# Turning x1 and x2 in the FP4 stage: TensorE transposes against a trip through DRAM and VectorE's square transposes

## The chip, the cores and the metric

The kernel runs on one core of a Trainium2 chip. The metric is the device time of one execution in microseconds (us). A separate profiled execution gives the trace. TensorE is called PE (its weight loads PEld), VectorE DVE, ScalarE ACT, GpSimd POOL; SP is the engine whose queue issues nearly all transfers.

## The reference

The program is two transformer layers on 2 x 1024 tokens of 512 channels, float32. Each layer adds an attention and a feed-forward part to x and normalizes after each. Cut to the part that the change touches:

```python
x = layernorm(x + linear_attention(x))            # gives x1
w_gu, w_dn = dequant(gate_up), dequant(down)      # 4-bit codes times fp16 scales of 128 inputs each
g, u = split(x @ w_gu.T)                          # 1408 features each
y = (silu(g) * u) @ w_dn.T
x = layernorm(x + y / rms(y))                     # gives x2
x = layernorm(x + gated_linear_attention(x))      # second layer
x = layernorm(x + top_k_ffn(x))
```

x1 enters the FP4 product, and x2 enters the second layer's products, with the channels on the partitions. The layer norms leave both with the tokens on the partitions. So both have to be turned.

## The kernel before, in words

Tokens are worked on in four blocks of 512, each four tiles of 128 tokens by 512 channels (`x_t[blk]`, in SBUF all the time). The program has stages, one after the other: the first attention (`s1`, to about 236 us of the trace), the FP4 feed-forward (to about 500 us), the second attention, and the top-k feed-forward.

**First attention.** The order of PE, DVE, ACT and POOL is made by a scheduler from the program's dependences. In the gaps the FP4 weights are unpacked: `unpack` issues a transfer of packed codes (`pk`, L267, two buffers), DVE shifts and masks them (L270, L271), and ACT writes them out as weights (`wgu`, `wdn`, L274). Each transfer waits until ACT has freed its buffer. `o_products(blk)` ends with the layer norm of a block; its last step, a subtraction and a multiplication per tile, runs on POOL (L222). Block 0's x1 is turned by PE inside this stage (`split_some`); that stays.

**FP4 feed-forward.** Here the order of PE, DVE, ACT and POOL is written out by hand (`manual_schedule`). The work is cut into chunks: chunk n is block n // 11 and a group n % 11 of 128 features, 44 in all. x1T is held as two float32r numbers, `x1Th` (rounded) and `x1Tl` (the remainder), and each 128-channel piece of a product is two matmuls, one with each (`in_two`, L928). A chunk has four pieces k for the gate and four for the up part. After each of the first three pieces the sum in PSUM is multiplied by a ratio of scales (L953 on ACT, L955 on DVE), and the next piece adds to it. The last piece of the gate goes through Silu (L957); the last of the up part is multiplied with it on DVE into `whole` (L959). POOL splits `whole` into `hhi` and `hlo` (L961, L962), which are the weights of the down product `yp`; after each group DVE multiplies `yp` by a ratio (L987).

Step n of the loop has two halves, and two chunks are in work at once. In each half PE runs, in this order: the older chunk's gate piece, the newer chunk's gate piece, the older chunk's up piece, the newer chunk's up piece (two matmuls each), and two `yp` products (four matmuls). A list `later` holds further work by step and half, which is issued after the `yp` products of that half: the row statistics and the norm of x2 (`Normed`, stats on DVE, norm on POOL), for the block that has just ended.

The dictionary `turned_in` names the steps in which PE turns a tile, in the second half, before the `yp` products: four transposes of 128 x 128 into a gate bank (`transposed`, L236). For x1 ACT then copies the rounded part (L250) and DVE subtracts it to get the remainder (L251): steps 4 to 7 for block 1, 17 to 20 for block 2, 28 to 31 for block 3. For x2 ACT copies the tile to xT (L1050): steps 22, 23, 32, 33 for block 0 and 34, 38, 39, 40 for block 1. Where a tile was turned, the next step's first half does the newer chunk's gate piece after the up pieces, since the bank is still in use. Blocks 1, 2 and 3 are first wanted by chunks 11, 22 and 33, in the first half of the step of that number.

**SP's queue** runs in the program's order; a transfer whose source or room isn't ready holds all behind it. Eight completion counters are used in turn, so a transfer also waits for the eighth one before it. At the end of `s1` SP issues the 11 broadcasts of the down ratios (`ratio`, L913).

Of the kernel before, what the change touches and what calls it, by code (L numbers as in the profile page):

```python
# [10 lines left out]
F32 = mybir.dt.float32  # L11
F32R = mybir.dt.float32r
F16 = mybir.dt.float16
# [8 lines left out]
P = 128  # L22
B, T, C = 2, 1024, 512
NB = 4
KC = C // P
I_FF = 1408
NI = I_FF // P
# [5 lines left out]
FG = 2 * NI  # L33
# [40 lines left out]
def body(ctx: ExitStack, tc: tile.TileContext, a: dict, out: bass.AP):  # L74
    nc = tc.nc
# [7 lines left out]
    dram = ctx.enter_context(tc.tile_pool(name="dram", bufs=1, space=DRAM))  # L83
# [9 lines left out]
    def mm_bank(name):  # L93
        return bank("mm", name)

    def acc_bank(name):
        return bank("acc", name)

    fp4 = ctx.enter_context(ExitStack())
    wfp4 = fp4.enter_context(tc.tile_pool(name="wfp4", bufs=1))  # L100
# [20 lines left out]
            wdn[i] = wfp4.tile([P, wdn_parts[i + 1] - wdn_parts[i], C], F32R, tag=f"wdn{i}", name=f"wdn{i}")  # L121
        return wdn[i][:, g - wdn_parts[i]]

    gus = wfp4.tile([KC * FG, P], F16, name="gus")
    scale = wfp4.tile([P, KC * FG], F32, name="scale")


# [2 lines left out]
    def const(name):  # L130
        at, n = _AT[name]
        return table[:, at : at + n]
# [3 lines left out]
    def place_w(i, name):  # L136
        return wpool.tile([P, KC, C], F32, tag=f"A{i}", name=name)
# [4 lines left out]
    x_t = [x[:, :, :C] for x in x_row]  # L142
# [4 lines left out]
    def xT_slot(i, name, dtype=F32):  # L147
        return xtp.tile([P, KC, 512], dtype, tag=f"xT{i}", name=name)

    def new_xT(blk):  # L150
        t = xT_slot(blk % 2, f"x0T{blk}")
        return t, a["xT"][:, blk * 512 : (blk + 1) * 512].rearrange("(k p) t -> p k t", p=P)
# [12 lines left out]
    t, src = new_xT(0)  # L165
# [15 lines left out]
    xT = {0: t}  # L181
# [33 lines left out]
    def layernorm(x, mv, eps=1e-5, by=nc.vector):  # L215

        n = x.shape[1]
        rs = sp.tile([P, 4], F32, tag="rs", name="rs")
        nc.vector.tensor_scalar_add(rs[:, :n], mv[:, :, 1], eps)  # L219
        power = nc.gpsimd.tensor_tensor(rs[:, :n], rs[:, :n], const("mhalf")[:, :n], ALU.pow).ins  # L220
        for i in range(n):
            by.tensor_scalar(x[:, i], x[:, i], mv[:, i, 0:1], rs[:, i : i + 1], ALU.subtract, ALU.mult)  # L222
        return power
# [8 lines left out]
    def transposed(x, name, room=mm_bank):  # L232

        pt = room(name)
        for k in range(KC):
            ins = nc.tensor.transpose(pt[:, k * P : (k + 1) * P], x[:, k * P : (k + 1) * P], ident).ins  # L236
        last_turned[0] = ins
        return pt

    def split_tiles(blk):  # L240

        i, j = ((2, 2), (1, 0), (0, 1), (2, 2))[blk]
        hi = xT_slot(i, "x1Th", F32R)
        lo = wpool.tile([P, KC, 512], F32R, tag=f"A{j}", name="x1Tl")
        return hi, lo

    def split_quarter(parts, blk, i, room=mm_bank):
        hi, lo = (t[:, :, i * P : (i + 1) * P] for t in parts)
        pt = transposed(x_t[blk][:, i], "x1Tp", room).rearrange("p (k t) -> p k t", k=KC)
        nc.scalar.copy(hi, pt)  # L250
        nc.vector.tensor_sub(lo, pt, hi.bitcast(F32))  # L251
# [7 lines left out]
    s1 = ctx.enter_context(ExitStack())  # L259
    wk = s1.enter_context(tc.tile_pool(name="s1", bufs=2))  # L260
    dq = s1.enter_context(tc.tile_pool(name="dq", bufs=2))

    def unpack(parts_, packed, n):

# [26 lines left out]
    def unpack_some(n):  # L291
        for _ in range(n):
            job = next(to_unpack, None)
            if job is not None:
                with tc.issue_after(anchor[0]):
                    unpack(*job)
# [46 lines left out]
    def behind():  # L343

        return ExitStack() if last_pe[0] is None else tc.issue_after(last_pe[0])
# [68 lines left out]
    tile_of = lambda i: slice(i * P, (i + 1) * P)  # L414
# [119 lines left out]
    def o_products(blk):  # L534

        A11, A12, A21, A22 = (qT[blk][:, 2 * e : 2 * e + 2, 256 * t : 256 * t + 256] for t in range(2) for e in range(2))
        G = G_of[blk // 2]
        B11, _, B21, B22 = (G[:, 2 * e : 2 * e + 2, 256 * o : 256 * o + 256] for e in range(2) for o in range(2))
        T1, T2, T3, T4 = TG[blk // 2]

        def product(ps, a, b, first, t, o):

            with behind():
                for r in range(2):
                    for k in range(2):
                        ins = nc.tensor.matmul(
                            ps[:, 256 * r : 256 * r + 256], a[:, k, r * P : (r + 1) * P], b[:, k],
                            start=first and r == 0 and k == 0, stop=k == 1, skip_group_check=True,
                        ).ins
            last_pe[0] = ins  # L550
            x = x_t[blk][:, 2 * t : 2 * t + 2, 256 * o : 256 * o + 256]
            return nc.vector.tensor_add(x, x, ps.rearrange("p (r c) -> p r c", r=2)).ins

        if blk not in S_of:
            q_sums(blk)
        S1, S2 = S_of[blk]
        grow = acc_bank("grow")
        added = product(grow, A11, B11, True, 0, 0)
        with tc.issue_after(added):
            for rest in TG_rest:  # L560
                rest()
            TG_rest.clear()
            nc.vector.tensor_sub(A21, A11, A21)
        yield
        product(acc_bank("P2"), A12, B21, True, 0, 0)
        yield
        product(grow, S2, T2, False, 1, 0)
        nc.vector.tensor_sub(A12, A12, S2)
        yield
        side = acc_bank("P7")  # L570
        product(side, A21, T3, True, 1, 1)
        yield
        product(grow, S1, T1, False, 1, 1)
        yield
        product(side, A22, T4, False, 1, 0)
        yield
        product(grow, A12, B22, False, 0, 1)
        yield
        mv = mv_of[blk] = sp.tile([P, 4, 2], F32, tag="mv", name="mv")
        with tc.issue_after(weighed[0]):  # L580
            for i in range(4):
                row_stats(mv[:, i], x_t[blk][:, i])
            layernorm(x_t[blk], mv, by=nc.gpsimd)
        yield

    def add_o(blk, i):
# [25 lines left out]
    first = [mm_bank("kp") for _ in range(4)]  # L612
# [60 lines left out]
    for b in range(B):  # L673
        i, j = 2 * b, 2 * b + 1
# [26 lines left out]
        split = [step(split_some, n) if b else [] for n in range(4)]  # L701
# [15 lines left out]
        more()  # L717
    late = mv_of[3]
    unpack_some(1000)
    sg = wk.tile([KC * FG, P], F32, name="sg", bufs=1)  # L720
    nc.gpsimd.tensor_copy(sg, gus)
    pg = mm_bank("pg")
# [20 lines left out]
    def xT_tile(name):  # L743
        return xT_slot(next(free), name)
# [164 lines left out]
    with tc.tile_pool(name="s2", bufs=1) as wk2:  # L909
# [22 lines left out]
        parts_of = {0: parts}  # L932
# [113 lines left out]
        def x2_tile(blk, i, name_bank):  # L1046
            if i == 0:
                xT[blk] = xT_tile("x2T")
            pt = transposed(x_t[blk][:, i], "x2Tp", name_bank)
            nc.scalar.copy(xT[blk][:, :, tile_of(i)], pt.rearrange("p (k t) -> p k t", k=KC))  # L1050

        def split(blk, i, name_bank):
            if i == 0:
                parts_of[blk] = split_tiles(blk)
            split_quarter(parts_of[blk], blk, i, name_bank)

        turned_in, later = {}, {}
        for blk in range(NB - 1):
            first = 4 if blk == 0 else NI * blk + 6
            for i in range(4):  # L1060
                turned_in[first + i] = lambda room, blk=blk, i=i: split(blk + 1, i, room)
        for n, (blk, i) in {22: (0, 0), 23: (0, 1), 32: (0, 2), 33: (0, 3), 34: (1, 0), 38: (1, 1), 39: (1, 2), 40: (1, 3)}.items():
            turned_in[n] = lambda room, blk=blk, i=i: x2_tile(blk, i, room)

        def add(n, half, job):
            later.setdefault((n, half), []).append(job)

        for b in range(NB - 1):
            n = NI * (b + 1)
            of = lambda f, b=b: lambda: f(normed[b])  # L1070
            add(n + 2, 1, of(lambda y: y.squares((0, 1))))
            add(n + 3, 0, of(lambda y: (y.squares((2, 3)), y.power())))
            add(n + 3, 1, of(lambda y: y.to_x((0,))))
            add(n + 4, 0, of(lambda y: y.to_x((1,))))
            add(n + 4, 1, of(lambda y: y.to_x((2,))))
            add(n + 5, 0, of(lambda y: y.to_x((3,))))
            for i in range(4):
                add(n + 5 + (i + 1) // 2, (i + 1) % 2, of(lambda y, i=i: y.stats(i)))
                add(n + 7 + i, 1, of(lambda y, i=i: y.norm(i)))
        for i in range(4):  # L1080
            add(3 + i, 1, lambda i=i: norm_tiles(3, late, (i,)))

# [8 lines left out]
            load_w(Wog, "WogT")  # L1091
            begin_gate()

        add(25, 1, load_gate)
        add(34, 0, load_other_gate)

        gates = Gates(gates_at[:3])
# [100 lines left out]
    wk = s3.enter_context(tc.tile_pool(name="s3", bufs=1))  # L1198
# [698 lines left out]
    wk = ctx.enter_context(tc.tile_pool(name="s4", bufs=2))  # L1897
# [4 lines left out]
    room = xT_tile("row")  # L1902
# [78 lines left out]
```

## Time and profile before

| what | value |
|---|---|
| runs of the kernel | 910.84, 910.49, 909.23 us, median 910.49 |
| the profiled execution | 908.87 us, of which the span of the trace is 907.0 us |
| busy in the span | PE 891.1, DVE 676.2, ACT 382.5, POOL 262.1 us |
| FP4 stage, 250 to 500 us | PE 250.0, DVE 192.0, ACT 190.8, POOL 136.5 us of 250 |
| granted PE clock | 0.997 on average, 1.00 from 0 to 850 us |
| a tile turned by PE | four transposes, 272 ns each by the record; 64 records each for x1T and x2T |

A row of the timeline has: start in us, length in us, engine, line, operation, output <- inputs, shape, how many instructions are merged in it, and in brackets how long the engine had been idle and what ended that. Instructions of an engine overlap: the distance between two starts is shorter than the length, and sums have to be made with the distances. Matmuls overlap most: a matmul of 512 columns is 0.39 us long in the record, and the next one starts 0.23 us later.

### The profile page before, as it was taken

The numbers are of one execution on the slowest core, as the hardware profiler recorded it, in microseconds if no ns is written. First come the engines' busy times: TensorE is split into PE (matmuls) and PEld (weight loads), VectorE is DVE, ScalarE is ACT, GpSimd is POOL, SyncE is SP. The second block draws the span as 40 slices with busy tenths as digits, with TensorE's granted clock in tenths as the row PEclk, the third lists the DMA queues.
The fourth block names the chain that finished last, engine by engine and source line by source line (L and its number), as shares of the span: only waits on it lengthen the run. The fifth ranks groups of instructions, "written<-read, shape, count | busy, mean of one in ns | idle before, by whom it ended". The sixth has DMA issues, their size and how long they took to land.

```text
span 907.0 us, 10985 instructions
## 1 busy us (share of the span) xinstructions
PE 891.1 (98%) x4035; PEld 698.6 (77%) x4035; DVE 676.2 (75%) x1304; ACT 382.5 (42%) x652; POOL 262.1 (29%) x229
## 2 busy tenths in 40 slices
PE   8999999999999999999999999999999999999996
PEld 6668886687688888888877677788585888888886
DVE  2569995589777787787769865857977986898535
ACT  2345343463476877877867434231201223120000
POOL 1020075200573456555654302020250030000112
PEclk9999999999999999999999999999999999999998
DMA  9632211200300001001001500000024220330001
GB/s 334 207 97 79 79 60 50 67 1 0 129 1 1 1 0 43 5 1 47 1 1 47 209 1 1 1 0 1 1 94 139 93 93 2 108 125 0 12 36 47
DMA packets 25992, 50.17 MB, mean 55 GB/s; under 512 B 4783, under 2 KB 5339, under 8 KB 25426
## 3 DMA queue, kind: packets, MB, share of 16 engines
q1 hardware_dynamic: 23441, 44.40, 14.4%
q0 software_dynamic: 1920, 4.22, 1.2%
q10 hardware_dynamic: 576, 0.85, 0.3%
q8 instruction: 32, 0.52, 0.2%
q14 instruction: 23, 0.18, 0.1%
HBM read 41.03 MB, written 10.54 MB: 57 GB/s over the span
## 4 chain that ended last, share of the span: by engine, by line
PE 83%; DVE 11%; ACT 2%; issue 2%; DMA 1%; POOL 0%; SPq 0%; POOLq 0%
PE yp L1664 10%; PE yp L928 9%; PE hp L1578 9%; PE gatep L928 8%; PE upp L928 8%; PE go L896 7%; PE xk L423 6%; PE grow L372 5%; PE P L372 3%; PE kp L617 2%; PE ao L591 2%; PE ao L1451 2%; PE grow L1417 1%; DVE cmp L1502 1%; PE op L1289 1%
## 5 line engine op out<-in xcount | busy, mean ns | idle before, releaser
L987 DVE TENSOR_TENSOR yp<-yp,ratio 128x512 f32<-128x512 f32 x160 | 103.3, 693 | 15.2 <-PE yp L928 15.0
L220 POOL TENSOR_TENSOR rs<-rs,table 128x4 f32<-128x4 f32 (+1 forms) x19 | 17.2, 904 | 294.4 <-DVE rs L219 294.2
L953 ACT ACTIVATE gatep<-gatep,scale 128x512 f32<-128x512 f32 x132 | 85.1, 656 | 34.9 <-PE gatep L928 32.2
L928 PE MATMUL yp<-wdn,hhi 128*128 128x512 f32 x176 | 71.8, 408 | 0.0
L928 PE MATMUL gatep<-x1Th,wgu 128*128 128x512 f32 x176 | 70.2, 399 | 0.0
L928 PE MATMUL yp<-wdn,hlo 128*128 128x512 f32 x176 | 69.8, 397 | 0.2 <-POOL hlo L962 0.2
L928 PE MATMUL gatep<-x1Tl,wgu 128*128 128x512 f32 x176 | 69.2, 393 | 0.3 <-DVE x1Tl L251 0.3
L928 PE MATMUL upp<-x1Tl,wgu 128*128 128x512 f32 x176 | 69.0, 392 | 0.0
L928 PE MATMUL upp<-x1Th,wgu 128*128 128x512 f32 x176 | 68.8, 391 | 0.0
L953 ACT ACTIVATE upp<-upp,scale 128x512 f32<-128x512 f32 x88 | 57.8, 661 | 11.1 <-PE upp L928 7.2
L962 POOL TENSOR_TENSOR hlo<-whole,hhi 128x512 fp32r<-128x512 f32 x43 | 55.6, 1292 | 3.5
L961 POOL CAST hhi<-whole 128x512 fp32r<-128x512 f32 x43 | 26.3, 612 | 99.8 <-DVE whole L959 98.7
L959 DVE SCALAR_TENSOR_TENSOR whole<-upp,scale,silu 128x512 f32<-128x512 f32 x43 | 32.3, 751 | 24.9 <-PE upp L928 18.6
L896 PE MATMUL go<-spare,spare 128*128 128x256 f32 x192 | 44.0, 381 | 0.0
L227 DVE BATCH_NORM_STATS2 st<-x 128x6 f32<-128x512 f32 x64 | 42.4, 678 | 0.4
L423 PE MATMUL xk<-pair,x 128*128 128x512 f32 x96 | 42.7, 592 | 0.0
L1311 POOL TENSOR_TENSOR sum<-sum,sq 128x512 f32<-128x512 f32 x12 | 18.2, 1519 | 77.1 <-issue 67.5
L896 PEld LDWEIGHTS go<-spare,spare 128*128 128x128 f32 x192 | 36.0, 190 | 5.8 <-issue 1.2
L928 PEld LDWEIGHTS gatep<-x1Th,wgu 128*128 128x128 f32 x176 | 33.1, 188 | 9.1 <-ACT gatep L953 1.1
L955 DVE TENSOR_SCALAR upp<-upp,scale 128x512 f32<-128x512 f32 x44 | 33.0, 752 | 9.1 <-PE upp L928 8.0
L928 PEld LDWEIGHTS yp<-wdn,hhi 128*128 128x128 f32 x176 | 33.1, 188 | 8.7 <-DVE yp L987 1.1
L928 PEld LDWEIGHTS gatep<-x1Tl,wgu 128*128 128x128 f32 x176 | 33.1, 188 | 8.0 <-DVE x1Tl L251 0.6
(468 smaller groups left out, 2107.2 us busy)
## 6 DMA issues: line engine op xcount, KB each, us to landing
pk<-in_gu SPq DMA_DIRECT2D x16, 352.0 KB, 3.7
x<-in_x SPq DMA_DIRECT2D x4, 1024.0 KB, 14.8
w<-in_w SPq DMA_DIRECT2D x1, 4096.0 KB, 12.3
xs<-picked SPq DMA_DIRECT2D x4, 1024.0 KB, 5.1
out<-x SPq DMA_DIRECT2D x4, 1024.0 KB, 4.2
w<-in_w SPq DMA_DIRECT2D x4, 1024.0 KB, 6.5
x0T<-in_xT SPq DMA_DIRECT2D x3, 1024.0 KB, 7.2
pk<-in_dn SPq DMA_DIRECT2D x11, 256.0 KB, 3.2
```

The lines of the kernel that those rows point to most:

```text
L227: nc.vector.bn_stats(st, x)
L372: ins = nc.tensor.matmul(ps[:, 256 * r : 256 * r + 256], a[:, k, r * P : (r + 1) * P], b[:, k], start=first and r == 0 and k == 0, stop=k ...
L423: ins = nc.tensor.matmul(acc_of[b][c], x_t[blk][:, i, c * P : (c + 1) * P], pairs_of["k", blk][i // 2][:, i % 2], start=blk % 2 == 0 and i ...
L896: ins = nc.tensor.matmul(ps[:, 256 * m : 256 * m + 256], w[:, k, m], b[:, k, 256 * half : 256 * half + 256], start=first and m == 0 and k ...
L928: nc.tensor.matmul(ps, w, x, start=start and n == 0, stop=stop and n == 1, skip_group_check=True)
L953: nc.scalar.activation(ps, ps, AF.Copy, scale=s)
L955: nc.vector.tensor_scalar(ps, ps, s, None, ALU.mult)
L959: nc.vector.scalar_tensor_tensor(self.whole, ps, s, self.silu, ALU.mult, ALU.mult)
L962: nc.gpsimd.tensor_sub(lo, self.whole, hi.bitcast(F32))
L987: nc.vector.tensor_tensor(self.y[:, i] if g == NI - 1 else ps, ps, ratio[:, g], ALU.mult)
L1578: ins = nc.tensor.matmul(ps[:, 256 * j : 256 * j + 256], pair_of(w, g)[:, k, j], x[:, k], start=k == 0, stop=k == 1).ins
L1664: nc.tensor.matmul(ps[:, 256 * r : 256 * r + 256], x(r, j), w(j), start=j == 0, stop=j == NJ - 1)
```

## The change

Twelve tiles of x1T (blocks 1, 2, 3) and eight of x2T (blocks 0, 1) are no longer turned by PE. `put_rows` writes the rows of a block or a tile to DRAM. `get_squares` reads them back with four transfers, one for each quarter of the partitions, such that partition 32 g + j holds, for each k and each group tr of 32 tokens, 32 channels in a row: runs of 128 bytes, 2048 runs in each transfer of a block, 512 in each of a tile. After that each 32 x 32 square lies where it belongs, but not turned; DVE's transpose of the squares turns all of a tile (128 x 512) in one instruction. x2 block 2 is still turned by PE after the loop, block 3 later.

x1T: DVE turns tile i (`turn_x1`), in the next step's first half ACT copies the rounded part (`high_part`), in its second half DVE makes the remainder (`low_part`, now from two operands in SBUF; before, one was in PSUM). The turns are in steps 5 to 8, 17 to 20 and 28 to 31, the last `low_part` in steps 9, 21 and 32. x2T: DVE turns straight into xT in steps 23 to 26 and 34 to 37; ACT has no part in it.

On SP's queue there are now: the write of block 1 (1 MB) behind the second of the 11 packed transfers of the down weights; two of the four reads of block 1, the write of block 2, and the other two reads ahead of the `ratio` broadcasts; then the write of block 3, the reads of blocks 2 and 3 as their rooms come free, and the writes and reads of the x2 tiles. `Wig`, whose room now holds squares, is loaded in step 33 and not 25. `gus` moves to a pool of the first stage. A step that turned a tile has the usual order again in the step after it.

```diff
+    def put_rows(blk, name, part=range(4)):
+        if (blk, name) not in rows_of:
+            rows_of[blk, name] = dram.tile([512, C], F32, name=f"{name}{blk}")
+        at, to = part[0], part[-1] + 1
+        nc.sync.dma_start(
+            out=rows_of[blk, name][P * at : P * to].rearrange("(c p) d -> p c d", p=P), in_=x_t[blk][:, at:to]
+        )
+    def get_squares(blk, name, room, part=range(4)):
+        at, to = part[0], part[-1] + 1
+        src = rows_of[blk, name][P * at : P * to].rearrange("(tr j) (k g i) -> g j k tr i", j=32, k=KC, g=4)
+        for g in range(4):
+            nc.sync.dma_start(out=room[32 * g : 32 * g + 32].rearrange("j k (tr i) -> j k tr i", i=32), in_=src[g])
...
             layernorm(x_t[blk], mv, by=nc.gpsimd)
+        if blk:
+            put_rows(blk, "x1r")
...
     unpack_some(1000)
+    squares = {1: xT_slot(0, "x1S")}
+    get_squares(1, "x1r", squares[1])
...
-        for blk in range(NB - 1):
-            first = 4 if blk == 0 else NI * blk + 6
-            for i in range(4):
-                turned_in[first + i] = lambda room, blk=blk, i=i: split(blk + 1, i, room)
-        for n, (blk, i) in {22: (0, 0), 23: (0, 1), 32: (0, 2), 33: (0, 3), 34: (1, 0), 38: (1, 1), 39: (1, 2), 40: (1, 3)}.items():
-            turned_in[n] = lambda room, blk=blk, i=i: x2_tile(blk, i, room)
+        def turn_x1(blk, i):
+            x1T[blk, i] = square_tile("x1T")
+            nc.vector.transpose(x1T[blk, i], squares[blk][:, :, tile_of(i)])
+        def high_part(blk, i):
+            if i == 0:
+                parts_of[blk] = split_tiles(blk)
+            nc.scalar.copy(parts_of[blk][0][:, :, tile_of(i)], x1T[blk, i])
+        def low_part(blk, i):
+            hi, lo = (t[:, :, tile_of(i)] for t in parts_of[blk])
+            nc.vector.tensor_sub(lo, x1T[blk, i], hi.bitcast(F32))
+        def turn_x2(blk, i):
+            if i == 0:
+                xT[blk] = xT_tile("x2T")
+            nc.vector.transpose(xT[blk][:, :, tile_of(i)], squares[blk, i])
+        for blk in range(1, NB):
+            first = 5 if blk == 1 else NI * blk - 5
+            for i in range(4):
+                add(first + i, 1, lambda blk=blk, i=i: turn_x1(blk, i))
+                add(first + i + 1, 0, lambda blk=blk, i=i: high_part(blk, i))
+                add(first + i + 1, 1, lambda blk=blk, i=i: low_part(blk, i))
+        add(8, 0, lambda: put_rows(3, "x1r"))
+        add(NI + 1, 0, lambda: get_x1(2))
+        add(2 * NI + 1, 0, lambda: get_x1(3))
+        for blk in range(2):
+            first = (23, 34)[blk]
+            for i in range(2):
+                add(first - 1, 0, lambda blk=blk, i=i: get_x2(blk, i))
+            for i in range(4):
+                add(first + i, 1, lambda blk=blk, i=i: turn_x2(blk, i))
+                if i < 2:
+                    add(first + i, 1, lambda blk=blk, i=i: get_x2(blk, i + 2))
...
+                if b < 2:
+                    add(n + 8 + i, 0, lambda b=b, i=i: put_rows(b, "x2r", (i,)))
...
-        add(25, 1, load_gate)
+        add(33, 0, load_gate)
```

More of the change, by code (lines that the diff above doesn't have):

```diff
@@ L122, in wdn_group @@
         return wdn[i][:, g - wdn_parts[i]]
-    gus = wfp4.tile([KC * FG, P], F16, name="gus")
     scale = wfp4.tile([P, KC * FG], F32, name="scale")
@@ L238, in transposed @@
         return pt
+    rows_of = {}
+    def put_rows(blk, name, part=range(4)):
[10 more added lines that the diff above has]
+            nc.sync.dma_start(out=room[32 * g : 32 * g + 32].rearrange("j k (tr i) -> j k tr i", i=32), in_=src[g])
     def split_tiles(blk):
@@ L261, in body @@
     dq = s1.enter_context(tc.tile_pool(name="dq", bufs=2))
+    gus = wk.tile([KC * FG, P], F16, name="gus", bufs=1)
     def unpack(parts_, packed, n):
@@ L1050, in x2_tile, with add, square_tile @@
             nc.scalar.copy(xT[blk][:, :, tile_of(i)], pt.rearrange("p (k t) -> p k t", k=KC))
-        def split(blk, i, name_bank):
+        turned_in, later = {}, {}
+        def add(n, half, job):
+            later.setdefault((n, half), []).append(job)
+        def square_tile(name):
+            return wk2.tile([P, KC, P], F32, tag="square", name=name, bufs=2)
+        x1T = {}
+        def turn_x1(blk, i):
+            x1T[blk, i] = square_tile("x1T")
+            nc.vector.transpose(x1T[blk, i], squares[blk][:, :, tile_of(i)])
@@ L1053, in split @@
+        def high_part(blk, i):
             if i == 0:
                 parts_of[blk] = split_tiles(blk)
-            split_quarter(parts_of[blk], blk, i, name_bank)
-        turned_in, later = {}, {}
-        for blk in range(NB - 1):
-            first = 4 if blk == 0 else NI * blk + 6
-            for i in range(4):
-                turned_in[first + i] = lambda room, blk=blk, i=i: split(blk + 1, i, room)
-        for n, (blk, i) in {22: (0, 0), 23: (0, 1), 32: (0, 2), 33: (0, 3), 34: (1, 0), 38: (1, 1), 39: (1, 2), 40: (1, 3)}.items():
-            turned_in[n] = lambda room, blk=blk, i=i: x2_tile(blk, i, room)
@@ L1065, in add, with get_x1, get_x2 @@
-        def add(n, half, job):
-            later.setdefault((n, half), []).append(job)
+            nc.scalar.copy(parts_of[blk][0][:, :, tile_of(i)], x1T[blk, i])
+        def low_part(blk, i):
+            hi, lo = (t[:, :, tile_of(i)] for t in parts_of[blk])
+            nc.vector.tensor_sub(lo, x1T[blk, i], hi.bitcast(F32))
+        def get_x1(blk):
+            squares[blk] = xT_slot(2, "x1S") if blk == 2 else place_w(0, "x1S")
+            get_squares(blk, "x1r", squares[blk])
+        def get_x2(blk, i):
+            squares[blk, i] = square_tile("x2S")
+            get_squares(blk, "x2r", squares[blk, i], (i,))
```

## The prediction

> **What bounds the kernel now.** I read the page's busy times first, then the stage's busy times in stretches of 50 us, then the timelines of single engines around one tile that PE turns, around one undisturbed step, and in the first attention where the new transfers enter SP's queue.
>
> ```profile
> PE 891.1 (98%) x4035; PEld 698.6 (77%) x4035; DVE 676.2 (75%) x1304; ACT 382.5 (42%) x652; POOL 262.1 (29%) x229
> ...
> 300.00:350.00 50.00, 50.00 (x226) 40.60 (x225) 39.69 (x65) 39.70 (x68) 28.75 (x28) 1.00 0.00 1
> ...
> 260.90 0.39 PE L928 MATMUL upp<-x1Tl,wgu 128*128 128x512 f32 x1
> 261.13 0.60 PE L236 MATMUL x1Tp<-table,x 128*128 128x128 f32 x4
> 261.48 0.48 PE L928 MATMUL yp<-wdn,hhi 128*128 128x512 f32 x1
> 261.80 0.40 PE L928 MATMUL yp<-wdn,hlo 128*128 128x512 f32 x1
> 262.03 0.40 PE L928 MATMUL yp<-wdn,hhi 128*128 128x512 f32 x1
> ```
>
> PE is the bound of the FP4 stage: 50.00 of 50 us, at a granted clock of 1.00, with no gap between starts. DVE has 39.69 of 50, POOL 28.75. So an instruction taken from PE there is time, as long as nobody makes PE wait. From 260.90 to 261.80 are 0.90 us, where two matmul distances of 0.233 would be 0.47: a turned tile costs PE 0.43 us. Whole steps say the same: DVE's `whole` comes every 5.54 us (279.00, 284.54), and every 5.98 where a tile is turned.
>
> **Part 1, gain: 20 tiles x 0.435 = 8.7 us.** All of it is on the path, since PE is.
>
> **Part 2, DVE's queue in the FP4 stage.** Rows of one undisturbed step, DVE, then POOL, then PE:
>
> ```profile
> 284.54 0.75 DVE L959 SCALAR_TENSOR_TENSOR whole<-upp,scale,silu 128x512 f32<-128x512 f32 x1 [0.70 <-PE upp L928]
> 285.30 1.30 DVE L987 TENSOR_TENSOR yp<-yp,ratio 128x512 f32<-128x512 f32 x2
> 287.15 0.76 DVE L955 TENSOR_SCALAR upp<-upp,scale 128x512 f32<-128x512 f32 x1 [0.56 <-PE upp L928]
> ...
> 286.05 1.29 POOL L962 TENSOR_TENSOR hlo<-whole,hhi 128x512 fp32r<-128x512 f32 x1
> ...
> 286.26 0.40 PE L928 MATMUL gatep<-x1Tl,wgu 128*128 128x512 f32 x1
> ...
> 128.69 1.75 DVE L328 SCALAR_TENSOR_TENSOR pair<-pair,e 128x512 f32<-128x512 f32 x1
> ...
> 128.12 1.77 POOL L442 TENSOR_TENSOR ksum<-ksum,pair 128x512 f32<-128x512 f32 x1
> ```
>
> From start to start DVE takes 0.66 for `whole` and the scaling, 0.605 for a `yp` product. The squares' transpose has no row. Below, the nearest is the mask of 128x512 int32 (0.41 apart), above, two passes of a f32 instruction (1.2). I take 0.60, the distance of the statistics: like the transpose, one f32 input of 512 columns, read from SBUF.
>
> The remainder (0.61) now has both inputs in SBUF. The last two rows show what that does: L328, with two SBUF inputs, is 0.69 long elsewhere, and here it ended 0.55 after POOL's sum of two SBUF tiles did. So DVE waited for POOL's instruction. `low_part` comes up behind `whole` and two products, at 285.30 + 1.21 = 286.51, and POOL's `hlo`, released by the same `whole`, runs to 287.34: a wait of 0.83. Bounds: 0, and 2.08 if POOL's norm of a tile gets in first. I take 0.83, since at 130.95 DVE came in at the first end of a POOL instruction with another behind it.
>
> (a) The last remainder of blocks 2 and 3 stands in the second half of steps 21 and 32; the fourth matmul of the very next half reads it. That is 286.26 in these rows; the remainder would end at 287.34 + 0.60 = 287.94 and be seen 0.05 later, so PE waits 1.73. DVE is also some 0.25 late from the step before (see b): 2.0 each, 4.0 in all. Without the wait for POOL it would be 0.95 each. In the kernel before, this remainder was made a step earlier. Block 1's comes two steps ahead: nothing.
>
> (b) A half with a remainder and a turn takes DVE 0.66 + 1.21 + 0.83 + 0.61 + 0.60 = 3.91, and the scaling that is queued behind them is due 2.61 after `whole`. It is 1.30 late; PE wants its result 1.35 after it is normally done (282.37 to 283.72). So one such half costs nothing. A step takes DVE 3.91 + 1.87 = 5.78 of 5.54, so 0.24 more is carried each time, for three steps: about 0.1, 0.3 and 0.3 where they add up, 0.7 for block 1. In blocks 2 and 3 two statistics of 0.81 each lie just before the first such half and make DVE some 0.6 later: 0.9 there and 0.1 after it, since PE's wait lets DVE catch up. Together 0.7 + 2 x 1.0 = 2.7.
>
> (c) The eight turns of x2 (0.60) lie alone in a half in which DVE has 2.77 - 1.87 = 0.90 to spare: nothing. Eight ACT copies (0.59) go; ACT has idle time behind every one, so nothing either.
>
> Part 2 together: 6.7.
>
> The Trainium skill (VectorE: DVE Perf Modes, The three transpose paths) gives DVE 311 ns for 128x128 in bf16, in 32x32 blocks, against TensorE's 390, and advises TensorE for a full transpose into PSUM; four of the 311 would be an estimate of 1.24 us for a tile, and the whole sum would then be the second rival's. No run here shows it.
>
> **Part 3, SP's queue in the first attention.** SP, DVE, ACT, POOL and PE around the place where the write of block 1 is put in:
>
> ```profile
> 139.68 10.53 POOL L222 TENSOR_SCALAR x<-x,mv,rs 128x512 f32<-128x512 f32 x4
> ...
> 142.67 1.28 SPq L267 DMA_DIRECT2D pk<-in_dn  x2
> ...
> 146.01 0.49 DVE L270 TENSOR_SCALAR pk<-pk,shift 128x512 int32<-128x512 int32 x1 [3.29 <-DMA pk<-in_dn]
> ...
> 152.05 0.58 ACT L399 COPY pair<-grow 128x512 f32<-128x512 f32 x1 [3.68 <-PE grow L372]
> ...
> 155.28 1.89 PE L372 MATMUL grow<-Wk,rw 128*128 128x256 f32 x8
> ...
> pk<-in_gu SPq DMA_DIRECT2D x1, 352.0 KB, 5.8
> ```
>
> The third packed transfer is issued at 142.67 and DVE already waits for it until 146.01. In the changed order the write of block 1 stands ahead of it, and that waits for POOL's norm, which ends at 150.21. With 0.4 for its own issue, the third transfer starts at 150.7. It lands after 3.2 us (the median of its kind) at best, or 5.8 as in the last row, where 1 MB was issued just before: I take 4.6, 155.3. DVE stands still until then, and behind it is the chain DVE shift 0.52, sum `rw` 0.60, mask 0.43, ACT's unpacking 0.53, ACT's copy of `pair` 0.58 (queued behind the unpacking), and PE's product of 155.28, which needs `rw` and the bank that this copy reads: 2.7 after the landing, 158.0. PE has nothing else: 2.7, with bounds 1.3 and 4.0. I add 0.3 for the next packed transfer, which is late too. Part 3: 3.0.
>
> **Part 4, other transfers, costed at nothing.** The nearest row to 128-byte runs is the load of `wqk`, 512 runs:
>
> ```profile
> 34.60:34.80 0.20, 0.20 (x2) 0.11 (x1) 0.17 (x1) 0.00 (x0) 0.00 (x0) 1.00 1.17 187
> ```
>
> At 187 GB/s a run takes 0.69 ns, a block's 8192 runs 5.6 us; over its whole 0.75 us it was 1.5 ns, 12 us. Blocks 2 and 3 have five steps, 27 us. The first `ratio` broadcast was issued at 236.62 and used at 247.56. Now POOL's norm of block 2 (to 237.43), a 1 MB write (4.2 as for `out`) and 4096 runs (2.8) come first; with its own shortest 3.2 it lands at 247.6 to 248.2, and PE returns to that bank at 249.58. Nothing, with little to spare. The reads of x2 tile 2 queue behind block 3's and have 17 us; they need 9 to 17. `Wig` has seven steps for 5.4 us. The Trainium skill (DMA: Bandwidth & Descriptors, Specifications) wants 512 bytes in a run for the full rate; by its ratio of overhead for small ones (3 cycles on 4) an estimate is 57% of the 390 GB/s of the trace's large loads, 4.7 us a block, and the sum stays as it is.
>
> **Sum:** -8.7 + 6.7 + 3.0 = +1.0 on the profiled execution's 908.87, 909.9. The median of the runs is 1.6 above that execution; the same on top gives 911.5.
>
> **Rivals.**
> 1. `low_part` doesn't wait for POOL. For it: in this stage no DVE row shows such a wait. Against it: the row at 128.69. Then (a) is 2 x 0.95 and (b) nearly nothing: part 2 is 2.1, the sum -3.6, 906.9.
> 2. Slower: the squares' transpose takes two passes, 1.2 from start to start. Each of the three steps a block with both instructions then carries 0.6 more, which PE pays: 9 x 0.6 = 5.4, 916.9. It decides from 0.70 on, where 9 x 0.10 lifts +1.0 to +1.9. For it: no row of the form; against it: all f32 forms with 512 columns are 0.60 to 0.66 apart.
> 3. Slower: 128-byte runs cut from rows of 2 KB go at half the slower rate (3 ns). `ratio` is then 5 to 9 late and x2 tile 2 some 10: +12 or more, 924. Against it: `wqk`.
> 4. The first attention absorbs its 3.0, as DVE idles 4.3 us at 152.74: 908.5. Against it: PE has no gap after 155.28 to win it back.
>
> **How the numbers follow.** The sum as it stands 0.54 (its own range 909.3 to 914), rival 1 0.14, rival 2 0.12, rival 3 0.10, rival 4 0.10. Some 0.2% (1.8 us) is what a measurement of this kernel can tell from no change: 908.7 to 912.3. Faster: rival 1 0.13, 0.07 of rival 4, 0.04 of the sum: 0.24. Slower: rivals 2 and 3 and 0.20 of the sum: 0.42. The same: the rest, 0.34. The range takes in most of rival 1 and rival 2 and leaves out rival 3: 906.4 to 917.5.
>
> **What would show it.** Right: no L236 rows from 250 to 500 except block 2's at the end; steps of 5.54 everywhere but at chunks 22 and 33, where PE waits some 2 us for DVE's `x1Tl`; waits of `upp` for the scaling in steps 18 and 29; remainders of 1.4 us in DVE's rows; a gap of 2 to 4 us in PE near 155. Wrong: remainders of 0.69, transposes of over 0.8, waits of DVE for `x1S`, `x2S` or `ratio`.

## The result, and the profile after

| | before | after |
|---|---|---|
| median of 20 runs each | 910.50 us (909.16 to 911.26) | 912.21 us (909.82 to 912.71) |
| ratio of the times | | 1.0017, 95% interval 1.0010 to 1.0024 |
| the profiled execution | 908.87 us, span 907.0 us | 912.31 us, span 910.5 us |
| from `grow<-Wq,x0T`, late in the first attention, to the first `yp` of the top-k part; the FP4 stage lies in it | 158.74 to 802.64: 643.90 us | 165.45 to 806.21: 640.76 us |

The kernel is 1.7 us slower (0.17%) where the sum said 1.0. The interval leaves out 1, so the loss is there, but it is smaller than the 0.2% up to which the prediction spoke of the same time. Of the 3.5 us between the two spans 2.56 us lie at the very start: the first `grow` starts at 22.01 and not at 19.45, before anything that was changed has run. In the kernels below this point lies between 19.76 and 22.73, with no relation to their edits. What is left is about +1.0 us: +4.15 us in the first attention and -3.14 us behind it.

The page of the changed kernel gives the busy times; stretches of its FP4 stage (PE, PEld, DVE, ACT, POOL busy, each with its number of instructions; granted PE clock; DMA share; GB/s) show where PE is no longer full:

```profile
PE 888.3 (98%) x3955; PEld 692.6 (76%) x3955; DVE 693.7 (76%) x1324; ACT 378.6 (42%) x644; POOL 263.4 (29%) x229
...
350.00:400.00 50.00, 48.40 (x208) 38.62 (x207) 42.14 (x65) 38.09 (x65) 29.50 (x28) 1.00 0.40 59
400.00:450.00 50.00, 48.06 (x206) 38.09 (x205) 43.62 (x68) 38.02 (x66) 29.31 (x26) 1.00 0.31 85
```

The 80 transposes are gone from PE (x3955 for x4035), DVE has 17.5 us more, and PE has 1.6 and 1.9 us without work in the two stretches that hold chunks 22 and 33. A step of block 1 with both a remainder and a turn, on DVE and then on POOL:

```profile
284.34 0.73 DVE L981 SCALAR_TENSOR_TENSOR whole<-upp,scale,silu 128x512 f32<-128x512 f32 x1
285.00 1.29 DVE L1009 TENSOR_TENSOR yp<-yp,ratio 128x512 f32<-128x512 f32 x2
286.19 1.48 DVE L1095 TENSOR_TENSOR x1Tl<-x1T,x1Th 128x512 fp32r<-128x512 f32 x1
287.60 0.70 DVE L1086 STREAM_TRANSPOSE x1T<-x1S 128x512 f32<-128x512 f32 x1
288.23 0.72 DVE L977 TENSOR_SCALAR upp<-upp,scale 128x512 f32<-128x512 f32 x1
...
285.83 1.30 POOL L984 TENSOR_TENSOR hlo<-whole,hhi 128x512 fp32r<-128x512 f32 x1
```

The transpose of the squares takes 0.63 from start to start (287.60 to 288.23). The remainder takes 1.41: it comes up at 286.19 while POOL's `hlo` runs to 287.13, and ends 0.54 after that. Ten of the twelve remainders take 1.39 to 1.49; the two at 348.20 and 412.00, where a norm has put POOL's `hlo` behind the remainder, take 0.77. The last remainder of block 2, and the matmul that reads it (PE, then DVE, then POOL), and all waits of PE from 250 to 500 us (what waited, for what, with the sum in us, the times, the longest):

```profile
358.90 0.39 PE L950 MATMUL gatep<-x1Th,wgu 128*128 128x512 f32 x1
360.89 0.50 PE L950 MATMUL gatep<-x1Tl,wgu 128*128 128x512 f32 x1 [1.60 <-DVE x1Tl L1095]
...
359.38 1.45 DVE L1095 TENSOR_TENSOR x1Tl<-x1T,x1Th 128x512 fp32r<-128x512 f32 x1
...
359.02 1.27 POOL L984 TENSOR_TENSOR hlo<-whole,hhi 128x512 fp32r<-128x512 f32 x1
360.27 2.51 POOL L1057 TENSOR_SCALAR x<-x,mv,rs 128x512 f32<-128x512 f32 x1
...
PE gatep L950 <- DVE x1Tl L1095: 3.2, 2, 1.6
PE upp L950 <- DVE upp L977: 0.7, 2, 0.3
PE yp L950 <- POOL hlo L984: 0.2, 1, 0.2
```

PE stands for 1.60 us; at 424.66 it does the same for block 3 (1.59). In the first attention, POOL, SP, DVE, ACT and PE:

```profile
142.22 9.09 POOL L221 TENSOR_SCALAR x<-x,mv,rs 128x512 f32<-128x512 f32 x4
...
151.33 0.37 SPq L246 DMA_DIRECT2D x1r<-x  x1
151.80 8.45 SPq L285 DMA_DIRECT2D pk<-in_dn  x3
...
157.59 0.49 DVE L288 TENSOR_SCALAR pk<-pk,shift 128x512 int32<-128x512 int32 x1 [12.33 <-DMA pk<-in_dn]
...
159.59 0.57 ACT L417 COPY pair<-grow 128x512 f32<-128x512 f32 x1
...
154.39 3.60 PE L441 MATMUL xk<-pair,x 128*128 128x512 f32 x8
160.21 3.68 PE L390 MATMUL grow<-Wk,rw 128*128 128x256 f32 x8 [2.22 <-ACT pair L417]
```

SP waits with the write until POOL's norm is done (151.3), the third packed transfer goes out behind it at 151.80 and lands at 157.5, DVE has stood still for 12.33 us, and PE has no work from 157.99 to 160.21. Then something comes that no step of the prediction had: eight matmuls that took 1.89 us take 3.68. The same place in stretches (columns as above; the granted clock is the last but two):

```profile
157.80:160.20 2.40, 0.19 (x1) 0.00 (x0) 1.82 (x4) 1.10 (x2) 0.00 (x0) 1.00 0.00 0
160.20:162.00 1.80, 1.79 (x4) 1.45 (x5) 0.69 (x1) 0.99 (x2) 0.00 (x0) 0.53 0.41 140
162.00:164.00 2.00, 2.00 (x7) 1.61 (x6) 1.59 (x4) 0.38 (x2) 0.00 (x0) 0.57 0.02 5
164.00:166.00 2.00, 2.00 (x11) 1.77 (x10) 1.31 (x2) 2.00 (x5) 0.00 (x0) 1.00 0.07 14
```

In the two stretches after the pause the granted clock is 0.53 and 0.57; it stands at 0.50 for 3.41 us, from 160.31 on. At half the clock these cost 1.7 us more.

### The profile page after: what moved, and what is told of

Same layout as the page of the kernel before. It is cut to its first block, busy times and chain, and to the rows that moved or that the text cites. A ratio compares the mean times of both kernels' runs of the same rounds, so it can differ in the third digit from the quotient of the medians.

```text
span 910.5 us, 10938 instructions
## 1 busy us (share of the span) xinstructions
PE 888.3 (98%) x3955; PEld 692.6 (76%) x3955; DVE 693.7 (76%) x1324; ACT 378.6 (42%) x644; POOL 263.4 (29%) x229
## 4 chain that ended last, share of the span: by engine, by line
PE 78%; DVE 13%; POOL 3%; issue 2%; ACT 2%; DMA 1%; POOLq 0%; SPq 0%; DVEq 0%; ACTq 0%
PE yp L1726 10%; PE hp L1640 9%; PE yp L950 8%; PE upp L950 8%; PE gatep L950 8%; PE go L918 7%; PE xk L441 5%; PE grow L390 4%; PE P L390 3%; PE kp L637 2%; PE ao L611 2%; PE ao L1513 2%; PE grow L1479 1%; DVE cmp L1564 1%; PE op L1351 1%
## 5 line engine op out<-in xcount | busy, mean ns | idle before, releaser
L950 PE MATMUL yp<-wdn,hhi 128*128 128x512 f32 x176 | 69.9, 397 | 0.0
L950 PEld LDWEIGHTS upp<-x1Th,wgu 128*128 128x128 f32 x176 | 33.0, 188 | 10.0 <-DVE upp L977 2.8
```

What stands on the lines that cost most here:

```text
L950: nc.tensor.matmul(ps, w, x, start=start and n == 0, stop=stop and n == 1, skip_group_check=True)
```

## The experiments

The theory: the gain of 8.7 us is there in full, and three things eat it: the place of the write on SP's queue (4.15), the place of the last remainder (two waits of PE), and DVE's lateness, for which the remainder's wait for POOL is the reason. How much of the stage each block loses is read from the starts of `whole`, chunk by chunk: 0.435 for each turn that PE no longer makes, less the time by which `whole` really comes earlier than before. Block 1 loses 0.44, block 2 2.64, block 3 2.57, together 5.65. The rivals: that the waits only move when they are removed, that the two-input form is long by itself, that a turn taken from PE is not worth 0.435.

**One part alone: x2T.** x1 is turned by PE and split from PSUM, as before:

```diff
-        if blk:
-            put_rows(blk, "x1r")
...
+        def split(blk, i, name_bank):
...
+            split_quarter(parts_of[blk], blk, i, name_bank)
+        for blk in range(NB - 1):
+            first = 4 if blk == 0 else NI * blk + 6
+            for i in range(4):
+                turned_in[first + i] = lambda room, blk=blk, i=i: split(blk + 1, i, room)
```

> Only x2T of blocks 0 and 1 goes through DRAM and VectorE's squares; x1T is turned by PE and the remainder is taken from PSUM, as before. The theory: eight turned tiles of 0.435 leave PE, and their turns lie in halves in which DVE has room: 910.5 - 3.5 = 907.0, 0.9962 of the kernel before. The rival, that DVE's turn or the transfers cost there what PE gains: 910.5, with PE waiting for upp in steps 23 to 26 and 34 to 37, or for x2T.

Measured: 908.03 us, ratio 0.9964 (0.9951 to 0.9978). From chunk 20 to chunk 43 the start of `whole` moves from 2.75 us later than before to 0.74 earlier: 3.49 for eight tiles, 0.436 each. PE waits for nothing of the change. So the unit of part 1 holds, and the turns and transfers of x2 cost nothing here.

**The remainder without POOL.**

```diff
-                    nc.gpsimd.tensor_sub(lo, self.whole, hi.bitcast(F32))
+                    if self.n not in (5, 6, 7, 8, 17, 18, 19, 20, 28, 29, 30, 31):
+                        nc.gpsimd.tensor_sub(lo, self.whole, hi.bitcast(F32))
...
-                add(n + 7 + i, 1, of(lambda y, i=i: y.norm(i)))
+                if b == 2:
+                    add(n + 7 + i, 1, of(lambda y, i=i: y.norm(i)))
```

> Left out of the computation: POOL's hlo of the twelve chunks whose second half holds a remainder, and the norm of x2 of blocks 0 and 1. POOL then has nothing to do when DVE comes to a remainder. The theory, that the remainder is long because DVE waits for POOL's instruction, gives 0.69 to 0.77 for all twelve remainders where they were up to 1.49; PE's wait for x1Tl falls from 1.6 to 0.8 each, and the lateness in the other halves goes: 912.2 - 1.6 - 1.4 = 909.2. The rival, that 1.45 is what the form with two inputs in SBUF takes by itself: remainders of 1.45 and 912.2.

Measured: 909.26 us, ratio 0.9984 (0.9975 to 0.9993). A remainder, from the timeline of DVE, and PE's wait for it from the list of its waits from 250 to 500 us:

```profile
285.99 0.68 DVE L1096 TENSOR_TENSOR x1Tl<-x1T,x1Th 128x512 fp32r<-128x512 f32 x1
...
PE gatep L950 <- DVE x1Tl L1096: 1.6, 2, 0.8
```

All twelve remainders take 0.68 to 0.75. PE's two waits halve, its waits for `upp` are gone, and the blocks now lose 0.07, 1.06 and 1.05, together 2.2. So the length is POOL's doing and not the form's, and it accounts for 3.5 of the 5.65. The Trainium skill (SBUF — State Buffer, Who interferes with whom) says that a DVE instruction with two SBUF inputs and a GpSimd instruction that reads SBUF exclude one another, whoever comes first; 1.48 against 0.68 is that rule in this trace. Its other side is there too: POOL's norm, 2.08 long, took 2.51 in the changed kernel where it met a remainder that had come first (360.27 above); with the remainders on POOL (below) it takes 2.08 in the same steps.

**The turns of blocks 2 and 3 one step earlier.**

```diff
-            first = 5 if blk == 1 else NI * blk - 5
+            first = 5 if blk == 1 else NI * blk - 6
```

> The turns of blocks 2 and 3 begin one step earlier, so that the last remainder is made a step before chunks 22 and 33 read it. The theory says that PE's two waits for x1Tl (1.6 us each) are the price of the place. They go, 3.2; but the statistics of two tiles now lie in the same halves as the first turn and the first remainder, which makes DVE some 0.8 later there, 2 x 0.8 = 1.6 at most. So 912.2 - 3.2 + 1.6 = 910.6, or down to 909.0 where the slack takes the statistics. The rival, that DVE as a whole is what the stage is short of and the waits only come elsewhere: 912.2, with as much waiting of PE for upp and gatep as there was for x1Tl.

Measured: 911.81 us, ratio 1.0010 (1.0001 to 1.0019). The waits for `x1Tl` are gone, but in the list of PE's waits from 250 to 500 us there is a new one:

```profile
PE upp L950 <- DVE upp L977: 3.7, 4, 1.1
```

Blocks 2 and 3 still lose 2.45 and 2.4. I had counted on 1.6 to 3.2 of gain, and 0.4 is what came: the turn, two statistics and a remainder of 1.49 lie in neighbouring halves, and the scaling behind them is late twice in each block. Here the rival was right: as long as a remainder costs DVE 1.4, the wait changes its place only.

**The remainders on POOL instead.**

```diff
-            nc.vector.tensor_sub(lo, x1T[blk, i], hi.bitcast(F32))
+            nc.gpsimd.tensor_sub(lo, x1T[blk, i], hi.bitcast(F32))
```

> All twelve remainders are made by POOL and not by DVE; nothing else is different from the changed kernel. Theory: DVE is no longer late in the halves with a turn (some 2.3 us of the stage go, no wait of PE for upp), and the last remainder of blocks 2 and 3 comes behind POOL's hhi and hlo, 0.75 + 1.3 + 1.3 = 3.35 after whole, where DVE ended it at about 1.2 + 1.45 = 3.4 after whole: PE's two waits of 1.6 stay. 912.2 - 2.3 = 909.9. Rival: POOL, with 1.3 more in steps that also hold a norm of 2.1, becomes late itself, and PE waits for hlo or x1Tl more than before: 912 or above.

Measured: 916.40 us, ratio 1.0065 (1.0052 to 1.0078), a miss: 6.5 us above what I expected. POOL's and PE's rows at the end of block 1, and the stretches around them:

```profile
356.44 2.08 POOL L1057 TENSOR_SCALAR x<-x,mv,rs 128x512 f32<-128x512 f32 x1
358.47 0.61 POOL L983 CAST hhi<-whole 128x512 fp32r<-128x512 f32 x1
359.17 1.26 POOL L984 TENSOR_TENSOR hlo<-whole,hhi 128x512 fp32r<-128x512 f32 x1
360.39 1.26 POOL L1095 TENSOR_TENSOR x1Tl<-x1T,x1Th 128x512 fp32r<-128x512 f32 x1
...
361.70 0.50 PE L950 MATMUL gatep<-x1Tl,wgu 128*128 128x512 f32 x1 [2.92 <-POOL x1Tl L1095]
...
361.70:363.00 1.30, 1.30 (x6) 1.08 (x7) 0.30 (x1) 0.66 (x1) 1.30 (x1) 1.00 0.31 49
363.00:366.50 3.50, 3.50 (x10) 2.75 (x9) 1.86 (x3) 1.35 (x2) 0.70 (x1) 0.51 0.67 150
366.50:369.00 2.50, 2.50 (x12) 2.02 (x12) 1.78 (x3) 1.43 (x3) 0.89 (x2) 1.00 0.20 33
```

With 1.3 more in a step that also holds the norm, POOL comes to `hhi` 0.8 late (`whole` ends at 357.65), and PE waits 2.92 for the remainder instead of 1.60. After each of the two pauses the clock is at half for 3.41 us, some 1.7 us more. So the rival was right on POOL, and the clock, which neither the theory nor the rival had, added more than half as much again to each pause: block 1, where no norm meets a remainder, loses nothing, blocks 2 and 3 lose 4.75 and 4.7.

**The place of the write on SP's queue.** In a first edit the call of `put_rows` for block 1 was moved down, just ahead of its reads:

```diff
-        if blk:
+        if blk > 1:
             put_rows(blk, "x1r")
...
+    put_rows(1, "x1r")
     squares = {1: xT_slot(0, "x1S")}
```

> The write of block 1 is issued just ahead of its reads, behind the last packed transfer of the down weights, and no longer ahead of the third. The theory is that this place alone costs the first attention what the trace of the changed kernel shows there: PE pauses 2.4 us at 157.8, and the granted clock is 0.53 to 0.57 for the next 4 us, some 1.8 us more. Then both go: no pause, a clock of 1.00 from 156 to 166, and 912.2 - 4.2 = 908.0, 0.9975 of the kernel before. First rival: the lower clock is not a consequence of the pause; then 912.2 - 2.4 = 909.8, and the clock is still low near 160. Second rival: the write only holds up something else, the reads or the ratio broadcasts behind it at 227 to 250; then the time stays at 912 and DVE waits for ratio.

Measured: 912.50 us, ratio 1.0018 (1.0008 to 1.0027), but the edit did not do what its expectation says. In this stage SP's order is made by the scheduler, and it put the write in its old place, between the second and the third packed transfer. So the run is a second sample of the changed kernel, and as such it is useful: PE's pause is there, and the clock does not fall (SP's and PE's timeline, and the next stretch):

```profile
128.93 7.91 SPq L285 DMA_DIRECT2D pk<-in_dn  x2
150.52 0.37 SPq L246 DMA_DIRECT2D x1r<-x  x1
...
159.33 1.99 PE L390 MATMUL grow<-Wk,rw 128*128 128x256 f32 x8 [2.17 <-ACT pair L417]
...
160.00:162.00 2.00, 2.00 (x11) 1.77 (x10) 0.64 (x2) 1.26 (x2) 0.00 (x0) 1.00 0.42 131
```

From the first `grow` to the `grow<-Wq,x0T` of the table it has 141.73 us, where the kernel before has 139.29 and the changed kernel's own profile 143.44. The pause alone is 2.44, with the low clock it is 4.15.

In the second edit the write is, on top of that, tied to the last packed transfer:

```diff
+        last_pk[0] = nc.sync.dma_start(out=pk, in_=src).ins
-        nc.sync.dma_start(out=pk, in_=src)
...
+    with tc.issue_after(last_pk[0]):
+        put_rows(1, "x1r")
     squares = {1: xT_slot(0, "x1S")}
```

> Now an order is forced on SP's queue: the write of block 1 stands behind all eleven packed transfers (185 us) and ahead of its reads (227 us). Theory: the first attention loses PE's pause of 2.2 to 2.4 us and nothing else is held up, so 912.2 - 2.3 = 909.9; where the low clock behind the pause (1.8 us) belongs to most runs, 908.0. The profile has no wait of PE for L417 near 158 and a clock of 1.00 from 156 to 166 in any case. Rival: the packed transfers, the reads of block 1 or the ratio broadcasts become late in its place; then 912 and a new wait of DVE or PE between 185 and 260.

Measured: 907.79 us, ratio 0.9976 (0.9967 to 0.9985), by the medians 4.4 us less than the changed kernel. SP's, then PE's rows:

```profile
127.52 50.47 SPq L287 DMA_DIRECT2D pk<-in_dn  x11
178.09 0.54 SPq L246 DMA_DIRECT2D x1r<-x  x1
...
155.59 1.89 PE L392 MATMUL grow<-Wk,rw 128*128 128x256 f32 x8
```

The eleven packed transfers run through, PE doesn't wait, the clock is 1.00, and the same distance is 139.29 again, to the last digit that of the kernel before. Nothing became late in its place. The gain in the medians is nearer to pause and low clock together (4.15) than to the pause alone (2.44), which speaks for both in most executions; the start, which differs by up to 3 us from profile to profile, is in these medians too.

**All three together**: the write behind the packed transfers, the turns a step earlier, the remainders on POOL.

> Three edits on the changed kernel: the write of block 1 behind the packed transfers, the turns of blocks 2 and 3 one step earlier, the remainders on POOL. If the pause in the first attention, the place of the last remainder and DVE's lateness are all that took the gain, then all of the 20 x 0.435 = 8.7 is left: 910.8 - 8.7 = 902.1, 0.9905 of the kernel before, up to 904 where the statistics make DVE late in the same halves as the first turn. Rival, that the turned tiles are worth less than that or that POOL becomes the limit: above 906, with waits of PE for POOL's hlo or x1Tl.

Measured: 902.42 us (901.87 to 904.74), ratio 0.9923 (0.9910 to 0.9936). Two stretches of the stage and PE's waits from 250 to 500 us:

```profile
350.00:400.00 50.00, 50.00 (x218) 40.42 (x216) 42.20 (x68) 39.86 (x69) 30.53 (x29) 1.00 0.36 55
400.00:450.00 50.00, 50.00 (x217) 40.48 (x216) 40.24 (x63) 40.05 (x69) 36.69 (x33) 1.00 0.32 85
...
PE yp L954 <- POOL hlo L988: 0.2, 1, 0.2
```

PE is full, and its only wait is one that the other kernels have as well. From chunk 0 to chunk 43 `whole` gains 8.82 on the kernel before, 20 x 0.441. This beats both kernels. Two of its edits gain next to nothing or lose by themselves: with DVE's remainders an earlier turn runs into the statistics, and POOL's remainders are only harmless once they have a step to spare. The three were not tried in pairs.

## Why the prediction was right

- **Part 1, 20 x 0.435 = 8.7.** Right: 0.436 a tile in the kernel with x2T alone, 8.82 in all with nothing in the way.
- **Part 2 (a), the last remainder: 2.0 each, 4.0.** The place, the reason and the two chunks were right. A wait is 1.60 of idle time, 1.76 between the starts: 3.5. The remainder ended 0.54 after POOL's instruction and not 0.60, and DVE came less late than the 0.25 that I added.
- **Part 2 (b), lateness: 0.7 + 2 x 1.0 = 2.7.** Measured 5.65 - 3.5 = 2.1: 0.44 in block 1 and about 0.8 each in blocks 2 and 3. Part 2 together 5.65 of 6.7. That the remainder would wait for POOL, which decided between the forecast and the first rival, is settled by the run without POOL: it lost 2.2 in the stage, and that rival had 2.1. The two remainders of 0.77, which met no `hlo`, were not in the forecast.
- **Part 2 (c), the x2 turns cost nothing.** Right, by the run of x2T alone.
- **The transpose, 0.60 taken between 0.41 and 1.2.** 0.63. The second rival, and the estimate of 1.24 from the Trainium skill (VectorE: DVE Perf Modes, The three transpose paths), were twice too high.
- **Part 3, 3.0 with bounds 1.3 and 4.0.** The chain was right link by link: write, norm, third transfer, DVE, ACT's copy, `grow<-Wk,rw`. The pause was 2.44 of lost time, for 2.7 and 0.3 in the sum. Here two errors nearly cancel: the landing took 5.7 and not the 4.6 that I took, but, counted from the first `grow`, the transfer was issued some 1.5 us earlier, since the last two tiles of POOL's norm took 2.07 and 2.06 where they took 2.31 and 3.27 before. What the term left out is what follows a pause: 1.7 of low clock. In the changed kernel's own profile it is 4.15, above its upper bound. The fourth rival (absorbed) is refuted.
- **Part 4, transfers at nothing.** Right: DVE waits for no `ratio`, `x1S` or `x2S`. Two of block 1's reads, 4096 runs, moved at 140 and 122 GB/s, about 1.0 ns for a run, between my 0.69 and 1.5. The third rival is refuted.
- **The sum.** -8.7 + 6.7 + 3.0 = +1.0; measured -8.8 + 5.65 + 4.15 = +1.0. That the two agree to a tenth is luck: part 2 was 1.05 too large and part 3 1.15 too small. The profiled execution itself took 912.31 where the sum gave 909.9; the 2.56 us of later start, which no term had, account for the difference of 2.4. And in the fifth profile, where the clock did not fall, the first attention lost 2.44 and not 4.15.

## What to carry to other kernels

A transfer whose source another engine has yet to finish should not stand ahead of others on a queue that issues in order: one write cost some 4 us, and the order that counts is the queue's in the built kernel, not that of the source. Before a step goes to the vector engine with two SBUF inputs, look at what GpSimd runs at that moment; before it goes to GpSimd, add up GpSimd's step; and give the result a step to spare. Where several edits block each other, test them together as well: here one gained 0.4 and another lost 4.2, and with the write moved they are the best kernel of all.

## What was not expected of the hardware

A short pause of PE in the middle of full work can cost twice. Of the pauses that these profiles show inside the steady stages, those of 1.59 to 1.60 us (six) were followed by a clock of 1.00. The pause of 2.14 to 2.22 us near 158 was followed by 3.41 us at half the clock in four of five profiles, and not in the fifth. Both pauses of 2.9 us were followed by it, once with 1.3 us at the full clock in between. So no length of a pause alone decides it here: in the first 12 us of the program two profiles have such a stretch, again 3.41 us, beside pauses of only 1.67 and 1.45 us. The Trainium skill (TensorE: Matmul & The Clock Gate, HAM oscillation) warns of pauses above about 3.4 us; here 2.2 was enough most times. That the same pause goes both ways would fit a window of activity that runs on its own time, as that page describes it, but no run here showed the window itself.
